# Routing list of a two-expert block: sums from TensorE, masks' inputs from ScalarE, fewer filler matmuls, and the accumulator filled from SBUF

## Chip, cores, metric

One NeuronCore of a Trainium2 chip (trn2). The metric is the device time in microseconds of one execution of the whole kernel; the time before is the median of three runs.

## What is computed

A block on x of 4 x 2048 tokens with 256 features: half a mixture of experts, attention, and half a mixture again.

```python
x = x + 0.5 * ffn(layernorm(x), router_w, wg, wu, wd)
x = x + attn(layernorm(x), Wq, bq, Wk, bk, Wv, bv, Wo, bo)
x = x + 0.5 * ffn(layernorm(x), router_w, wg, wu, wd)

def ffn(x, ...):                       # N = 8192 tokens, E = 8 experts, 2 per token
    capacity = int(1.25 * N / E)       # 1280 places per expert
    probs = softmax(xf @ router_w.T)
    topw, topi = top_k(probs, 2);  topw = topw / (topw.sum(-1) + 1e-6)
    order = lexsort((-fw, fe))         # by expert, the largest weight first
    rank = arange(2 * N) - starts[se]
    keep = rank < capacity
    disp[e, rank] = xf[token]          # kept tokens only
    eo = (silu(disp @ wg) * (disp @ wu)) @ wd
    out[token] += eo[e, rank] * weight * keep
```

The diff works on the step that says which tokens an expert keeps, and in which place of its list each stands.

## The kernel before

Each of the two mixtures runs in the same order: router, routing, lists, experts. The first mixture's router (`first_router`, L1156) runs over 16 groups of four tiles of 128 tokens: TensorE turns x and forms the logits, VectorE takes the statistics, GpSimd raises the variances to the power -0.5. `wrx`, the router's weights, is cleared by GpSimd (L1221) and filled by VectorE (L1232) ahead of the statistics on VectorE's queue. `choose` (L191) then takes each token's two experts, and writes their weights and factors into the columns behind x in `xw`. `write_rows` (L257) stores `xw` as `rows`, from which the experts gather.

`route` (L260) lays the weights of all experts out as 128 partitions of 512 tokens, 16 partitions to an expert (`wt`). Thirty rounds (L288 to L300) find each expert's smallest kept weight `cand` bit by bit: VectorE counts, TensorE sums the counts over the expert's partitions, VectorE takes the next value. What follows is a chain:

- L304 and L305 mark the tokens equal to the last kept weight (`tie`) and above it (`above`), and count both in each partition (`parts`).
- L307 and L308: TensorE sums the counts over the expert (`group`) and over its partitions further ahead (`ahead`).
- L310 scans the ties. L313 to L316 turn the sums into `need_t`, how many ties this partition keeps, and `off`, where its places begin.
- L317 to L320 drop the ties that have no place, scan what is kept, and make `St`, the place of each token.
- L323 `stay_busy` (L158): 14 calls of filler matmuls of 128 columns, whose result nobody reads. TensorE works in order, so L326, which turns `St` back to token-major, stands behind them.
- L328 to L335 split the place into `slot_hi` and `slot_lo`; L336 makes `behind_lo` on GpSimd, which ScalarE uses for the masks of the lists of experts 1 to 7.

The list of expert 0 is waited for (`RowList` with `waited_for`, L338). `high` (L351) compares `slot_hi` with 16 values (`hi`, L357) and multiplies by the row within the tile and by the tile (`hv`, L364 and L365), all on VectorE. `low` (L379) compares `slot_lo` with 128 values, eight tiles at a time (L384). TensorE multiplies the two (L396), ScalarE copies the sum (L404), TensorE turns it (L412), VectorE makes the indices, and GpSimd gathers the first rows (L470). The experts then keep TensorE busy to the end of the mixture, two chunks of 640 tokens to an expert.

In the first mixture `route` also carries other work between its rounds: the sums of expert 0's weights on GpSimd and the attention's weights.

The order of TensorE, VectorE and ScalarE is that of the program (`manual_schedule`); GpSimd's too, except among the experts. SP's queue is filled by a scheduler. Around the first routing it holds: 16 loads of x, expert 0's weights, the attention's weights, four copies of x to `acc` in HBM (L1245, 128 pieces of 64 KB), expert 1's weights, and the four writes of `rows` (L258). The experts add their results to `acc`. `hi` and `hv` take memory that `xw` gives up, so they wait for the writes of `rows`, which read it.

Of the kernel before, what the change touches and what calls it, by code (L numbers as in the profile page):

```python
# [9 lines left out]
F32 = mybir.dt.float32  # L10
F16 = mybir.dt.float16
# [16 lines left out]
def macaron_kernel(  # L28
# [103 lines left out]
    nc.gpsimd.memset(short, -(CAP - 1.0) / (P // E))  # L132
    minus_half = const.tile([P, 1], F32, name="minus_half")
    nc.gpsimd.memset(minus_half, -0.5)

    wr = const.tile([E, D], F32, name="wr")
    nc.scalar.dma_start(out=wr, in_=router_w)
# [122 lines left out]
    def route(w, pool, ppool, beside=iter(())):  # L260

        FULL = [P, GT * P]

        def new(name, dtype=F32):
            return pool.tile(FULL, dtype, name=name)

        def one(name, dtype=F32, n=1):
            return pool.tile([P, n], dtype, name=name)  # L270

        ps = ppool.tile([P, GT, P], F32, tag="turn", name="turn", bufs=1)
        by_group = w.rearrange("p e (g r) -> p r (e g)", r=GT)
        for r in range(GT):
            nc.tensor.transpose(ps[:, r, :], by_group[:, r, :], ident)
        wt = new("wt")
        nc.vector.tensor_copy(wt, ps.rearrange("p r q -> p (r q)"))

        cand, low, high = one("cand", I32), one("low", I32), one("high", I32)
        cand_f = cand.bitcast(F32)
        part = one("part", F16)
        above, tie = new("above", F16), new("tie", F16)
        nc.vector.memset(cand, 1 << 29)
        for bit in range(29, -1, -1):

            reach = ppool.tile([P, 4], F32, tag="cnt", name="reach", bufs=2)
            nc.tensor.matmul(reach[:, :1], group4, short, start=True, stop=False)  # L290
            nc.vector.tensor_scalar(above, wt, cand_f, 0.0, ALU.is_ge, ALU.add, accum_out=part)  # L291
            nc.tensor.matmul(reach[:, :1], group4, part, start=False, stop=True)
            next(beside, None)

            half = 1 << (bit - 1) if bit else 0
            nc.vector.tensor_scalar(low, cand, (1 << bit) | half, None, ALU.bitwise_xor)
            nc.vector.tensor_scalar(high, cand, half, None, ALU.bitwise_xor)
            nc.vector.tensor_scalar(  # L298
                cand_f, reach[:, :1], low.bitcast(F32), high.bitcast(F32), ALU.max, ALU.min
            )  # L300


        parts = one("parts", F16, 2)
        nc.vector.tensor_scalar(tie, wt, cand_f, 0.0, ALU.is_equal, ALU.add, accum_out=parts[:, 1:2])  # L304
        nc.vector.tensor_scalar(above, wt, cand_f, 0.0, ALU.is_gt, ALU.add, accum_out=parts[:, 0:1])  # L305
        cnt = ppool.tile([P, 4], F32, tag="cnt", name="all", bufs=2)
        nc.tensor.matmul(cnt[:, 0:1], group, parts[:, 0:1], start=True, stop=True)  # L307
        nc.tensor.matmul(cnt[:, 1:3], ahead, parts, start=True, stop=True)  # L308
        St = new("St")
        nc.vector.tensor_tensor_scan(St, row_of_ones, tie, 0.0, ALU.mult, ALU.add)  # L310
        nums = one("nums", n=3)
        need, need_t, off = (nums[:, k : k + 1] for k in range(3))
        nc.vector.tensor_scalar(need, cnt[:, 0:1], -1.0, float(CAP), ALU.mult, ALU.add)  # L313
        nc.vector.tensor_tensor(off, cnt[:, 2:3], need, ALU.min)
        nc.vector.tensor_tensor(need_t, need, cnt[:, 2:3], ALU.subtract)
        nc.vector.scalar_tensor_tensor(off, off, float(-1 - NOWHERE), cnt[:, 1:2], ALU.add, ALU.add)  # L316
        nc.vector.scalar_tensor_tensor(tie, St, need_t, tie, ALU.is_le, ALU.mult)  # L317
        nc.vector.tensor_tensor(above, above, tie, ALU.add)
        nc.vector.tensor_tensor_scan(St, row_of_ones, above, 0.0, ALU.mult, ALU.add)
        nc.vector.scalar_tensor_tensor(St, St, off, above, ALU.add, ALU.mult)  # L320


        stay_busy(ppool.tile([P, GT, P], F32, tag="turn", name="turn", bufs=1)[:, 0, :], 14, P)  # L323
        ps = ppool.tile([P, GT, P], F32, tag="turn", name="back", bufs=1)
        for r in range(GT):
            nc.tensor.transpose(ps[:, r, :], St[:, r * P : (r + 1) * P], ident)  # L326
        slot = pool.tile([P, E * T], I16, name="slot")
        nc.vector.tensor_scalar(  # L328
            slot.rearrange("p (q r) -> p q r", r=GT), ps.rearrange("p r q -> p q r"),
            float(NOWHERE), None, ALU.add,  # L330
        )
        nc.vector.tensor_scalar(
            slot_hi.rearrange("p e t -> p (e t)"), slot, 7, None, ALU.logical_shift_right
        )
        nc.vector.tensor_scalar(slot_lo.rearrange("p e t -> p (e t)"), slot, P - 1, None, ALU.bitwise_and)  # L335
        nc.gpsimd.tensor_scalar(behind_lo, slot_lo, -1.0, 0.5, ALU.mult, ALU.add)  # L336

    class RowList:  # L338

# [11 lines left out]
        def high(self):  # L351
            hi = self.pool.tile([P, T * HI], F16, tag="hi", name="hi", bufs=1)
            hv = self.pool.tile([P, 2 * T * HI], F16, tag="hv", name="hv", bufs=1)
            at = slot_hi[:, self.e, :]
            if self.waited_for:
                shape = [P, HI, T // TG, TG]
                nc.vector.tensor_tensor(  # L357
                    hi.rearrange("p (i g t) -> p i g t", g=T // TG, t=TG),
                    spread(counts[:, :HI, :].unsqueeze(2), shape),
                    spread(at.rearrange("p (g t) -> p g t", t=TG).unsqueeze(1), shape), ALU.is_equal,  # L360
                )
                hv = hv.rearrange("p (k i t) -> p k i t", k=2, t=T)
                shape, hi = [P, HI, T], hi.rearrange("p (i t) -> p i t", t=T)
                nc.vector.tensor_scalar(hv[:, 0, :, :], hi, row_in, None, ALU.mult)  # L364
                nc.vector.tensor_tensor(hv[:, 1, :, :], hi, spread(row_of.unsqueeze(1), shape), ALU.mult)  # L365
                self.hv = hv.rearrange("p k i t -> p t k i")
            else:
                shape, hi = [P, T, HI], hi.rearrange("p (t i) -> p t i", i=HI)
                nc.vector.tensor_tensor(
                    hi, spread(count[:, :HI].unsqueeze(1), shape), spread(at.unsqueeze(2), shape), ALU.is_equal  # L370
                )
                self.hv = hv.rearrange("p (t k i) -> p t k i", k=2, i=HI)
                nc.vector.tensor_scalar(self.hv[:, :, 0, :], hi, row_in, None, ALU.mult)
                nc.vector.tensor_tensor(self.hv[:, :, 1, :], hi, spread(row_of.unsqueeze(2), shape), ALU.mult)
# [837 lines left out]
    with tc.tile_pool(name="w1", bufs=2) as wpool:  # L1212
        weights, ws = {}, {}
        with tc.tile_pool(name="r1", bufs=1) as pool, tc.tile_pool(name="r1p", bufs=2, space=PSUM) as ppool:
# [5 lines left out]
            with tc.manual_schedule(engines=ENGINES):  # L1220
                nc.gpsimd.memset(wrx, 0.0)  # L1221
                ps = ppool.tile([P, DC, P], F32, tag="turn", name="wrT", bufs=1)
                for c in range(DC):
                    nc.tensor.transpose(ps[:, c, :E], wr[:, c * P : (c + 1) * P], ident[:E, :E])
                wrT = pool.tile([P, DC, E], F32, name="wrT")
                nc.vector.tensor_copy(wrT, ps[:, :, :E])
                ps = ppool.tile([P, DC, P], F32, tag="turn", name="means", bufs=1)
                for c in range(DC):
                    nc.tensor.matmul(ps[:, 0, :E], ones, wrT[:, c, :], start=(c == 0), stop=(c == DC - 1))
                mean = pool.tile([P, E], F32, name="wr_mean")  # L1230
                nc.vector.tensor_scalar(mean, ps[:, 0, :E], 1.0 / D, None, ALU.mult)
                nc.vector.tensor_tensor(  # L1232
                    wrx[:, :, :E], wrT, spread(mean.unsqueeze(1), [P, DC, E]), ALU.subtract
                )
                steps = attention_weights(pool, ppool)
                next(steps)
                first_router(xw, w, pool, ppool)
                for b in range(B):
                    write_rows(xw, rows[0], slice(b * NJ, (b + 1) * NJ))
                steps = chain(weight_sums(nc.gpsimd, 0, wpool, weights, ws, 0, 1), steps)  # L1240
                route(w, pool, ppool, steps)
                for _ in steps:
                    pass
        for b in range(B):
            nc.sync.dma_start(out=acc[b * N : (b + 1) * N, :], in_=x_in[b])  # L1245
        load_expert(1, wpool, weights)

        with tc.tile_pool(name="f1", bufs=1) as pool, tc.tile_pool(name="f1p", bufs=2, space=PSUM) as ppool:
# [55 lines left out]
```

## Time and profile before

| | |
|---|---|
| median of three runs | 1992.83 us (1991.80 to 1993.83) |
| the profiled execution's own time | 1991.23 us |
| its span | 1989.5 us |
| mean granted TensorE clock | 0.960 |
| first routing, from `choose` to the first gather | 35.5 to 110.8 us |
| second routing, to its first gather | to 1196.9 us |

Times within the profile count from the start of the span, in microseconds. PE is TensorE, PEld its weight loads, DVE VectorE, ACT ScalarE, POOL GpSimd, SP the queue that issues most DMAs. In the timeline a line gives start, duration, engine, line of the kernel, operation, output and inputs; in brackets stands how long the engine was idle before it, and what is taken to have released it. An f32 filler call appears as two matmuls.

### The profile page before, as it was taken

How to read it: one execution, taken by the hardware profiler on the slowest of the kernel's cores; microseconds unless marked ns; L12 is line 12 of the kernel's file. 1: busy time of each engine (PE TensorE's matmuls, PEld its weight loads, DVE VectorE, ACT ScalarE, POOL GpSimd, SP SyncE). 2: the span in 40 equal slices, each digit the busy share in tenths (PEclk: the TensorE clock that was granted, in tenths of full speed). 3: DMA queues.
4: the chain of work that ended last, by engine and by line, in shares of the span. 5: the costliest groups of instructions: out<-in, count | busy, mean ns of one | idle time of the engine just before them, and what ended most of it. 6: DMA issues, size and time to landing. Idle time of an engine off the chain costs nothing.

```text
span 1989.5 us, 25361 instructions
## 1 busy us (share of the span) xinstructions
PE 1843.9 (93%) x8812; PEld 1341.8 (67%) x8812; DVE 1386.9 (70%) x2539; ACT 922.4 (46%) x2269; POOL 1031.8 (52%) x1019
## 2 busy tenths in 40 slices
PE   6479999999999999999999528999999999999997
PEld 5347777777777777777888425777777777777776
DVE  7856767676767676647788885676767666676763
ACT  5045455555646463325444105554646373737332
POOL 4335555555555555535556324555555555555552
PEclk8589999999999999999999858999999999999999
DMA  9911323222222221125012541222222223232121
GB/s 339 332 30 28 92 34 86 59 61 71 50 71 49 71 50 28 28 25 172 25 40 89 187 142 29 71 50 71 49 71 50 71 50 79 41 95 30 31 29 19
DMA packets 99936, 148.85 MB, mean 75 GB/s; under 512 B 7512, under 2 KB 86368, under 8 KB 99680
## 3 DMA queue, kind: packets, MB, share of 16 engines
q1 hardware_dynamic: 69072, 103.29, 15.3%
q0 software_dynamic: 30720, 43.93, 13.8%
q8 instruction: 70, 1.15, 0.3%
q14 instruction: 58, 0.48, 0.1%
q10 hardware_dynamic: 16, 0.01, 0.0%
HBM read 99.49 MB, written 56.10 MB: 78 GB/s over the span
## 4 chain that ended last, share of the span: by engine, by line
PE 88%; DVE 6%; issue 3%; POOL 1%; ACT 1%; DMA 1%; POOLq 0%; DVEq 0%; ACTq 0%; SPq 0%
PE mm L561 49%; PE mm L764 23%; PE qp L949 2%; PE pc L1004 2%; PE tr L496 2%; PE py L1062 2%; PE back L716 2%; DVE above L291 2%; PE ix L396 1%; PE mm L822 1%; PE tr L1168 1%; DVE cand L298 1%; PE trq L992 1%; PE trx L941 1%; PE lg L1177 0%
## 5 line engine op out<-in xcount | busy, mean ns | idle before, releaser
L561 PE MATMUL mm<-xs,ws 128*128 128x320 f32 x1536 | 476.9, 433 | 2.8 <-DVE u L502 1.8
L505 POOL TENSOR_TENSOR ct<-ct 128x320 f32<-128x320 f32 x360 | 339.6, 943 | 187.9 <-DVE ct L592 164.4
L561 PEld LDWEIGHTS mm<-xs,ws 128*128 128x128 f32 x1536 | 284.3, 190 | 111.9 <-DVE u L502 2.9
L502 DVE TENSOR_TENSOR ct<-u,mm 128x640 f32<-128x640 f32 x256 | 209.9, 820 | 177.2 <-PE mm L561 166.0
L502 DVE TENSOR_TENSOR ct<-ct,mm 128x640 f32<-128x640 f32 x288 | 236.0, 819 | 73.7 <-PE mm L561 72.8
L470 POOL DMA_INDIRECT r<-rows,ixs x160 | 156.9, 981 | 235.2 <-ACT eo L697 172.8
L764 PE MATMUL mm<-ct,wds 128*128 128x320 f32 x960 | 278.1, 432 | 0.0
L589 ACT ACTIVATE ct<-ct 128x960 f32<-128x960 f32 (+2 forms) x192 | 141.7, 738 | 293.1 <-DVE ct L502 293.1
L390 ACT ACTIVATE lo<-from_below,behind_lo 128x129 f16<-128x129 f32 x896 | 272.9, 396 | 0.0
L764 PEld LDWEIGHTS mm<-ct,wds 128*128 128x128 f32 x960 | 179.2, 190 | 72.0 <-DVE ct L502 3.3
L764 PE MATMUL mm<-ct,wdt 128*128 128x320 f32 x720 | 213.5, 433 | 0.0
L698 POOL DMA_INDIRECT acc<-eo,ixs x80 | 127.7, 1596 | 142.9 <-ACT eo L697 124.9
L698 POOL DMA_INDIRECT out_dram<-eo,ixs x80 | 127.6, 1595 | 142.9 <-ACT eo L697 124.9
L561 PE MATMUL mm<-xsT,wgt 128*128 128x320 f32 x512 | 184.8, 443 | 0.0
L561 PE MATMUL mm<-xsT,wut 128*128 128x320 f32 x512 | 180.7, 435 | 0.0
L592 DVE TENSOR_TENSOR ct<-ct 128x640 f32<-128x640 f32 (+1 forms) x128 | 160.8, 1256 | 21.7 <-ACT ct L589 21.7
L502 DVE TENSOR_TENSOR u<-p,mm 128x640 f32<-128x640 f32 x128 | 105.1, 821 | 93.0 <-PE mm L561 80.6
L764 PEld LDWEIGHTS mm<-ct,wdt 128*128 128x128 f32 x720 | 132.1, 190 | 47.5
L561 PE MATMUL mm<-xsT,ws 128*128 128x320 f32 x512 | 158.7, 432 | 0.0
L598 ACT COPY p<-mm 128x640 f32<-128x640 f32 x128 | 88.4, 690 | 147.1 <-PE mm L561 147.1
L697 ACT ACTIVATE eo<-back,r 128x256 f32<-128x256 f32 x150 | 64.9, 478 | 152.7 <-PE back L716 152.7
L561 PEld LDWEIGHTS mm<-xsT,wut 128*128 128x128 f32 x512 | 97.7, 191 | 40.7 <-issue 0.8
(234 smaller groups left out, 2803.7 us busy)
## 6 DMA issues: line engine op xcount, KB each, us to landing
wgt<-in_L_ffn_wg_dram SPq DMA_DIRECT2D x16, 1024.0 KB, 4.9
wut<-in_L_ffn_wu_dram SPq DMA_DIRECT2D x16, 1024.0 KB, 7.2
wdt<-in_L_ffn_wd_dram SPq DMA_DIRECT2D x16, 1024.0 KB, 5.4
rows<-xw SPq DMA_DIRECT2D x7, 2240.0 KB, 19.4
xw<-in_L_attn_x_dram SPq DMA_DIRECT2D x16, 512.0 KB, 9.3
out_dram<-xw SPq DMA_DIRECT2D x16, 512.0 KB, 2.9
xw<-acc SPq DMA_DIRECT2D x15, 512.0 KB, 8.6
r<-rows,ixs POOLq DMA_INDIRECT x160, 2.8
```

Of the source, the lines that this page charges most:

```text
L291: nc.vector.tensor_scalar(above, wt, cand_f, 0.0, ALU.is_ge, ALU.add, accum_out=part)
L390: nc.scalar.activation(lo[:, t, :], from_below, AF.Sign, bias=at, scale=1.0)
L470: nc.gpsimd.indirect_dma_start(out=r, out_offset=None, in_=src[:, :], in_offset=bass.IndirectOffsetOnAxis(ap=lists[e][:, i : i + 1], axis=0),)
L502: nc.vector.tensor_tensor(o, a, b, op)
L505: nc.gpsimd.tensor_tensor(o, a, b, op)
L561: nc.tensor.matmul(ps, a, b, start=start, stop=True, skip_group_check=not start)
L589: nc.scalar.activation(h(p)[:, qs, :], h(p)[:, qs, :], AF.Silu)
L592: engine.tensor_tensor(h(p)[:, qs, :], h(p)[:, qs, :], hT(p)[:, qs, :], ALU.mult)
L598: nc.scalar.copy(p1, ps)
L697: nc.scalar.mul(eo, ps, got[k][i][:, D + e : D + e + 1])
L698: ins = nc.gpsimd.indirect_dma_start(out=dst[:, :], out_offset=bass.IndirectOffsetOnAxis(ap=lists[e][:, i0 + i : i0 + i + 1], axis=0), in_ ...
L764: nc.tensor.matmul(ps, a(p), b(p), start=(p == 0 and not more), stop=(p == NF - 1), skip_group_check=more)
```

## The change

- TensorE forms `need_t` and the start of the places outright: six one-column matmuls with negated matrices and constant columns instead of two. VectorE copies both numbers out and corrects `off` once.
- `stay_busy` makes 8 calls instead of 14.
- `behind_lo` and the first product of `hv` for the waited-for list go to ScalarE.
- `acc` is filled from `xw` in SBUF, in rows of 1 KB, instead of from x in HBM; on SP's queue these four DMAs keep their place, behind them come the four writes of `rows`, and then expert 1's weights.
- GpSimd makes five more constants at the start, ahead of `wrx`.

```diff
+    a_half = const.tile([P, 1], F32, name="a_half")
+    nc.gpsimd.memset(a_half, 0.5)
+    cap_part = const.tile([P, 1], F16, name="cap_part")
+    nc.gpsimd.memset(cap_part, CAP * E / float(P))
+    nowhere_part = const.tile([P, 1], F16, name="nowhere_part")
+    nc.gpsimd.memset(nowhere_part, (-1.0 - NOWHERE) * E / P)
+    minus_group = const.tile([P, P], F16, name="minus_group")
+    nc.gpsimd.tensor_scalar(minus_group, heads, -1.0, None, ALU.mult)
+    minus_ahead = const.tile([P, P], F16, name="minus_ahead")
+    nc.gpsimd.tensor_scalar(minus_ahead, ahead, -1.0, None, ALU.mult)
...
-        cnt = ppool.tile([P, 4], F32, tag="cnt", name="all", bufs=2)
-        nc.tensor.matmul(cnt[:, 0:1], group, parts[:, 0:1], start=True, stop=True)
-        nc.tensor.matmul(cnt[:, 1:3], ahead, parts, start=True, stop=True)
+        cnt = ppool.tile([P, 2], F32, tag="cnt", name="all", bufs=2)
+        for k, sums in enumerate((
+            ((group, cap_part), (minus_ahead, parts[:, 1:2]), (minus_group, parts[:, 0:1])),
+            ((group, nowhere_part), (ahead, parts[:, 1:2]), (ahead, parts[:, 0:1])),
+        )):
+            for n, (a, b) in enumerate(sums):
+                nc.tensor.matmul(cnt[:, k : k + 1], a, b, start=(n == 0), stop=(n == 2))
         St = new("St")
         nc.vector.tensor_tensor_scan(St, row_of_ones, tie, 0.0, ALU.mult, ALU.add)
-        nums = one("nums", n=3)
-        need, need_t, off = (nums[:, k : k + 1] for k in range(3))
-        nc.vector.tensor_scalar(need, cnt[:, 0:1], -1.0, float(CAP), ALU.mult, ALU.add)
-        nc.vector.tensor_tensor(off, cnt[:, 2:3], need, ALU.min)
-        nc.vector.tensor_tensor(need_t, need, cnt[:, 2:3], ALU.subtract)
-        nc.vector.scalar_tensor_tensor(off, off, float(-1 - NOWHERE), cnt[:, 1:2], ALU.add, ALU.add)
+        nums = one("nums", n=2)
+        need_t, off = (nums[:, k : k + 1] for k in range(2))
+        nc.vector.tensor_copy(nums, cnt)
         nc.vector.scalar_tensor_tensor(tie, St, need_t, tie, ALU.is_le, ALU.mult)
         nc.vector.tensor_tensor(above, above, tie, ALU.add)
+        nc.vector.scalar_tensor_tensor(off, need_t, 0.0, off, ALU.min, ALU.add)
         nc.vector.tensor_tensor_scan(St, row_of_ones, above, 0.0, ALU.mult, ALU.add)
         nc.vector.scalar_tensor_tensor(St, St, off, above, ALU.add, ALU.mult)
-        stay_busy(ppool.tile([P, GT, P], F32, tag="turn", name="turn", bufs=1)[:, 0, :], 14, P)
+        stay_busy(ppool.tile([P, GT, P], F32, tag="turn", name="turn", bufs=1)[:, 0, :], 8, P)
...
-        nc.gpsimd.tensor_scalar(behind_lo, slot_lo, -1.0, 0.5, ALU.mult, ALU.add)
+        nc.scalar.activation(behind_lo, slot_lo, AF.Identity, bias=a_half, scale=-1.0)
...
-                nc.vector.tensor_scalar(hv[:, 0, :, :], hi, row_in, None, ALU.mult)
+                nc.scalar.mul(hv[:, 0, :, :], hi, row_in)
...
                 first_router(xw, w, pool, ppool)
+                for t in range(0, T, NJ):
+                    nc.sync.dma_start(out=acc_tiles[:, t : t + NJ, :], in_=xw[:, t : t + NJ, 0:D])
                 for b in range(B):
                     write_rows(xw, rows[0], slice(b * NJ, (b + 1) * NJ))
...
-        for b in range(B):
-            nc.sync.dma_start(out=acc[b * N : (b + 1) * N, :], in_=x_in[b])
         load_expert(1, wpool, weights)
```

## The prediction

> **What bounds the kernel now.** I read the page's busy times and chain first, then the chain of waits and the timeline of the two stretches where the diff works, then the busy times by stage for clock and DMA.
>
> The page:
> ```profile
> PE 1843.9 (93%) x8812; PEld 1341.8 (67%) x8812; DVE 1386.9 (70%) x2539; ACT 922.4 (46%) x2269; POOL 1031.8 (52%) x1019
> PE 88%; DVE 6%; issue 3%; POOL 1%; ACT 1%; DMA 1%; POOLq 0%; DVEq 0%; ACTq 0%; SPq 0%
> ```
> TensorE carries 88% of the chain, but the experts and the attention, where it does, are not touched. The diff acts in the two routings, where VectorE and its hand-overs carry the chain. So the whole prediction is made in two stretches of some 15 us.
>
> The timeline of the first routing (start, duration, engine, line):
> ```profile
> 92.07 6.16 PE L161 MATMUL turn<-row_of_ones,ident 128*128 128x128 f32 x28
> 93.01 0.13 DVE L313 TENSOR_SCALAR nums<-all 128x1 f32<-128x1 f32 x1
> 93.44 0.74 DVE L317 SCALAR_TENSOR_TENSOR tie<-St,nums,tie 128x512 f16<-128x512 f32 x1
> 95.94 0.75 DVE L320 SCALAR_TENSOR_TENSOR St<-St,nums,above 128x512 f32<-128x512 f32 x1
> 98.29 0.66 PE L326 MATMUL back<-ident,St 128*128 128x128 f32 x4
> 98.98 0.69 DVE L328 TENSOR_SCALAR slot<-back 128x512 int16<-128x512 f32 x1 [2.29 <-PE back L326]
> 99.92 0.29 DVE L335 TENSOR_SCALAR slot_lo<-slot 128x512 int16<-128x512 int16 x1
> 100.29 0.62 POOL L336 TENSOR_SCALAR behind_lo<-slot_lo 128x512 f32<-128x512 int16 x1 [28.60 <-DVE slot_lo L335]
> 100.95 0.69 DVE L357 TENSOR_TENSOR hi<-counts,slot_hi 128x1024 f16<-128x1024 int16 x1 [0.75 <-POOL behind_lo L336]
> 101.68 0.49 DVE L364 TENSOR_SCALAR hv<-hi,row_in 128x1024 f16<-128x1024 f16 x1
> 102.08 0.69 DVE L365 TENSOR_TENSOR hv<-hi,row_of 128x1024 f16<-128x1024 f16 x1
> 103.42 4.93 PE L396 MATMUL ix<-lo,hv 128*32 128x128 f16 x64 [4.48 <-DVE lo L384]
> ```
> Two gaps. St is ready at 96.69, but the back transposes begin at 98.29, behind the 14 filler calls, which end at 98.23. And hi waits 0.75 us, by the label for GpSimd. The second routing corrects that label:
> ```profile
> 1180.18 4.88 PE L161 MATMUL turn<-row_of_ones,ident 128*128 128x128 f32 x28
> 1184.06 0.75 DVE L320 SCALAR_TENSOR_TENSOR St<-St,nums,above 128x512 f32<-128x512 f32 x1
> 1185.13 0.66 PE L326 MATMUL back<-ident,St 128*128 128x128 f32 x4
> 1187.13 1.18 POOL L336 TENSOR_SCALAR behind_lo<-slot_lo 128x512 f32<-128x512 int16 x1 [26.69 <-DVE slot_lo L335]
> 1187.13 0.69 DVE L357 TENSOR_TENSOR hi<-counts,slot_hi 128x1024 f16<-128x1024 int16 x1
> 1189.84 4.91 PE L396 MATMUL ix<-lo,hv 128*32 128x128 f16 x64 [4.06 <-DVE lo L384]
> ```
> Here hi starts together with behind_lo, so it does not wait for it. It waits for the rows' writes, whose source xw gives up the memory that hi takes: the last of the four was issued at 81.1 and took 19.7 us, so it landed at 100.8. The busy times by stage (PEclk, DMA share and GB/s are the last three columns) agree:
> ```profile
> 97.00:98.00 1.00, 1.00 (x7) 1.00 (x6) 0.00 (x0) 0.00 (x0) 0.00 (x0) 0.54 1.12 339
> 98.00:99.00 1.00, 0.89 (x6) 0.46 (x5) 0.02 (x1) 0.00 (x0) 0.00 (x0) 1.00 0.95 288
> 100.00:100.25 0.25, 0.00 (x0) 0.00 (x0) 0.20 (x2) 0.00 (x0) 0.00 (x0) 1.00 0.14 45
> ```
> The DMA engines run full to 99 us and are empty soon after 100: in the first routing a DMA backlog is the last gate.
>
> **The change, part by part.**
>
> *Numbers.* Four small VectorE operations between 93.01 and 93.44 become one copy. L313 to its dependent took 0.17, so tie starts 0.26 earlier. The new min/add (one column) sits between the sum into above and the second scan; such operations stood 0.07 to 0.11 apart, so +0.08. Net -0.18 per routing. TensorE's two one-column matmuls become six with six weight loads; two need nothing that is late, the other four at 0.1 us (a load of such weights) end about 92.6, under the first scan, which runs to 93.1.
>
> *Filler.* 14 calls made 28 matmuls of 0.22 us at half clock. Eight make 16, 3.5 us: from about 92.4 to 95.9, before St at 96.51. So the back transposes wait for St alone and start at 96.58. Their own time depends on the clock. At full clock four took 0.66. At half clock one took 0.47 and three 0.90 (L496 at 114.58 and 118.12), so four take 0.47 + 3 x 0.215 = 1.12. In the trace the grant came 5.9 us after the filler began in the first routing (97.9) and 3.2 us after it in the second (1183.4). [...]
>
> First routing: slot at 96.58 + 1.12 + 0.03 = 97.73 instead of 98.98, -1.25. Second: St at 1184.63, back at 1184.70, slot at 1185.85 instead of 1185.82, +0.03, since the early grant there had almost emptied the filler by itself.
>
> *The DMAs.* The four acc copies (8.4 MB) read SBUF instead of HBM in the same place of SP's queue, behind the attention weights (from about 37 us). The rows' four writes (9.2 MB) now stand ahead of expert 1's weights (3.15 MB). At the 345 GB/s that the rows' writes show, acc takes 24.3 us and the rows 26.6: they land at 88; taking 3.15 MB off the old landing gives 91.7. Both are well ahead of hi. With slot to hi 1.31 us as in the second routing, hi starts at 99.04 instead of 100.95: -1.91 in all there. The weights behind are done by 97 to 101, ahead of the gathers (108.6) and some 100 us ahead of expert 1. The rows also no longer wait for anything that is later than before: on SP they are passed by nothing.
>
> *ScalarE.* behind_lo leaves GpSimd, where nobody waited for it; on ScalarE it costs 0.72 (0.29 fixed with a per-partition operand, L390, plus 512 elements at 0.83 ns, L220), beside hi. hv's first product leaves VectorE. It stood 0.40 us on the path in the first routing and 0.65 in the second, where behind_lo ran on GpSimd at the same time and both were slower (0.73 against 0.49, 1.18 against 0.62). On ScalarE it takes 0.29 + 1024 x 0.83 ns = 1.14 from the end of hi, to hi + 1.9; VectorE's own path (hi, the other product, the first mask) lets TensorE start at hi + 2.07. The weight load must follow ScalarE by up to 0.3, so the bounds of the new wait are 0 and 0.15; I take 0.10. Behind the waiting load stand only the list's matmuls, which need it anyway; nothing else is due on ScalarE. From hi to the first ix matmul: 2.17 instead of 2.47 and 2.71.
>
> *GpSimd's set-up.* Five more operations ahead of wrx's memset: three at 0.03 and two of the 0.55 kind (L130), 1.2 us. wrx then comes at 7.9; TensorE's first use is at 8.41. VectorE's statistics shift by 1.2, rstd's last power from 33.7 to 34.9, and it is needed at 35.46. Cost nothing; without that cover 1.2.
>
> **Sum.** First routing: ix at 99.04 + 2.17 = 101.21 instead of 103.42, -2.21. Second: 1187.16 + 2.17 = 1189.33 instead of 1189.84, -0.51. Together -2.7 against the profiled execution: 1991.23 - 2.7 = 1988.5. That execution is 1.6 us below the median. Part is the lucky grant in the second routing: with the filler's end anywhere between 1184.87 (St) and 1186.34 (all at half clock), the usual one is some 0.5 later than the 1185.06 seen, and the changed kernel is free of that. So against the median -3.2: **1989.6 us**. The rest of the 1.6 I leave as scatter.
>
> **Rivals.**
> - *The clock is granted all the same* in both routings: another -0.92, 1988.7. For it: 3.2 us sufficed at 1183.4. Against: 5.9 at 97.9.
> - *The DMA gate stays*: the rows still land near 100.8. Then the first routing gains only 0.40 - 0.10, the second 1.0 with the 0.5 above: 1991.5. For it: the DMA engines have no free time before 99. Against: 3.15 MB leave the queue ahead.
> - *Slower: acc's writes in 1 KB pieces are slow.* They replace copies with 64 KB pieces, and the rows queue behind them. At half of 345 GB/s acc takes 48.7 us, the rows land at 112.4, hi waits until then, 11.6 later than before; less 1.3 gained elsewhere, 2003. It turns into a loss below about 210 GB/s (landing after 104). Against: the rows' 1.1 KB writes ran at 345.
> - *The set-up's cover is gone*: +1.2, 1990.8.
>
> **Numbers.** Forecast 0.54, clock granted 0.24, gate stays 0.11, cover gone 0.05, slow writes 0.06. The range takes in the first four with the runs' own scatter of 1 us: 1987.8 to 1992.0. Over 0.2% (4.0 us, about what a measurement can tell from no change) faster needs most of the clock case or scatter on the forecast: 0.33; slower 0.06; within 0.61.
>
> **What would show it.** In the changed profile: filler ended before St, back starting 0.07 behind it and taking 1.12 (0.66 in the rival); rows landed by 92 us and no wait ahead of hi; 2.1 to 2.2 from hi to ix in both routings; wrx later but ex still at 35.5. A gain outside the two routings, or hi still waiting at 100.9, would prove me wrong.

## The result and the profile after

The changed kernel takes **1987.85 us** (median of 11 runs, 1986.57 to 1988.22), the kernel before 1992.83 in 11 runs beside it (1990.70 to 1993.83): 0.9976 times, with the interval 0.9968 to 0.9984, or 5.0 us less. The prediction was 1989.6, with a range of 1987.8 to 1992.0: the result lies 0.05 us inside its lower end.

The profiled execution took 1988.04 us with a span of 1986.1. Its page, by the lines that were shown of before:
```profile
PE 1841.3 (93%) x8796; PEld 1338.2 (67%) x8796; DVE 1385.2 (70%) x2533; ACT 926.9 (47%) x2273; POOL 1030.9 (52%) x1022
PE 87%; DVE 8%; issue 2%; ACT 1%; POOL 1%; DMA 1%; POOLq 0%; DVEq 0%; ACTq 0%; SPq 0%
```
Little shows here: six VectorE instructions less, four more on ScalarE. 5 us of 1990 have to be looked for in the routings. The timeline of the first (the code around it stands 12 to 16 lines lower than before):
```profile
92.00 3.76 PE L173 MATMUL turn<-row_of_ones,ident 128*128 128x128 f32 x16
92.89 0.14 DVE L331 COPY nums<-all 128x2 f32<-128x2 f32 x1
93.06 0.75 DVE L332 SCALAR_TENSOR_TENSOR tie<-St,nums,tie 128x512 f16<-128x512 f32 x1
95.57 0.75 DVE L336 SCALAR_TENSOR_TENSOR St<-St,nums,above 128x512 f32<-128x512 f32 x1
96.47 1.09 PE L342 MATMUL back<-ident,St 128*128 128x128 f32 x4 [0.71 <-DVE St L336]
97.59 0.69 DVE L344 TENSOR_SCALAR slot<-back 128x512 int16<-128x512 f32 x1 [1.27 <-PE back L342]
98.90 0.72 ACT L352 ACTIVATE behind_lo<-slot_lo,a_half 128x512 f32<-128x512 int16 x1 [18.79 <-DVE slot_lo L351]
99.00 0.69 DVE L373 TENSOR_TENSOR hi<-counts,slot_hi 128x1024 f16<-128x1024 int16 x1 [0.19 <-DVE slot_lo L351]
99.73 0.69 DVE L381 TENSOR_TENSOR hv<-hi,row_of 128x1024 f16<-128x1024 f16 x1
99.78 1.15 ACT L380 ACTIVATE hv<-hi,row_in 128x1024 f16<-128x1024 f16 x1
100.97 0.46 PEld L412 LDWEIGHTS <-hv 128*32 128x32 f16 x9 [3.83 <-ACT hv L380]
101.07 4.92 PE L412 MATMUL ix<-lo,hv 128*32 128x128 f16 x64 [3.52 <-DVE lo L400]
```
Both gaps of before are gone. The filler ends at 95.76, ahead of `St`; `back` is released by `St` and nothing else; `hi` (99.00) starts behind `slot_lo` with no wait for memory. ScalarE's two operations lie beside VectorE's, and ix is released by VectorE's first mask `lo`, not by ScalarE. There is no room left, though: ix needs `hv` as weights, and their load, which waited for ScalarE, came at 100.97, 0.10 ahead of ix (0.03 in the second routing).

The second routing:
```profile
1177.88 3.76 PE L173 MATMUL turn<-row_of_ones,ident 128*128 128x128 f32 x16
1181.44 0.75 DVE L336 SCALAR_TENSOR_TENSOR St<-St,nums,above 128x512 f32<-128x512 f32 x1
1182.34 1.08 PE L342 MATMUL back<-ident,St 128*128 128x128 f32 x4 [0.70 <-DVE St L336]
1184.77 0.69 DVE L373 TENSOR_TENSOR hi<-counts,slot_hi 128x1024 f16<-128x1024 int16 x1
1186.85 4.92 PE L412 MATMUL ix<-lo,hv 128*32 128x128 f16 x64 [3.42 <-DVE lo L400]
```
The same picture: `back` behind `St` at half clock, ix 2.08 behind `hi`. The busy times by stage in the first routing (PEclk, DMA share and GB/s are the last three columns) answer to those of before:
```profile
95.00:96.00 1.00, 0.76 (x4) 0.46 (x3) 0.96 (x2) 0.00 (x0) 0.00 (x0) 0.50 0.77 245
96.00:97.00 1.00, 0.53 (x3) 0.56 (x4) 0.32 (x1) 0.00 (x0) 0.00 (x0) 0.50 0.10 32
97.00:98.00 1.00, 0.55 (x3) 0.15 (x1) 0.41 (x1) 0.00 (x0) 0.00 (x0) 0.50 0.00 0
```
The DMA engines are nearly empty from 96 on and empty from 97, expert 1's weights included; before, they were full to 99. The granted clock stays at 0.50.

For the comparison I measure each routing from its first scan of `St` (L310, now L328) to its first ix matmul, so that nothing from ahead of it is counted: 11.54 and 9.84 us before, 9.32 and 9.22 after.

### The profile page after: what moved, and what is told of

Read it like the earlier page. It is cut to its first block, busy times and chain, and to the rows that moved or that the text cites. A ratio compares the mean times of both kernels' runs of the same rounds, so it can differ in the third digit from the quotient of the medians.

```text
span 1986.1 us, 25337 instructions
## 1 busy us (share of the span) xinstructions
PE 1841.3 (93%) x8796; PEld 1338.2 (67%) x8796; DVE 1385.2 (70%) x2533; ACT 926.9 (47%) x2273; POOL 1030.9 (52%) x1022
## 4 chain that ended last, share of the span: by engine, by line
PE 87%; DVE 8%; issue 2%; ACT 1%; POOL 1%; DMA 1%; POOLq 0%; DVEq 0%; ACTq 0%; SPq 0%
PE mm L577 49%; PE mm L780 23%; DVE above L303 2%; PE qp L965 2%; PE pc L1020 2%; PE tr L512 2%; PE py L1078 2%; PE back L732 2%; PE ix L412 1%; PE mm L838 1%; DVE cand L310 1%; PE tr L1184 1%; PE reach L304 0%; PE trq L1008 0%; DVE st L1090 0%
```

## Experiments

None of these kernels leaves out work that the result needs, and one adds work that nobody reads. They ran on three chips. The experts' stages took 1494.2 to 1494.4 us in the profiles of before and after and in those of one chip (after_again, undo_filler, weights_first, undo_scalar), taken from the third `u` of a mixture to its last, or to the end, and 1497.3 to 1498.1 in those of the two others, whatever the kernel. So times of different chips are not set side by side; ratios are, each against the kernel before on the same chip. The table at the end of this section has all of them.

**The DMA part alone**, on the kernel before: `acc` from `xw`, and `rows` ahead of expert 1's weights.
```diff
                 first_router(xw, w, pool, ppool)
+                for t in range(0, T, NJ):
+                    nc.sync.dma_start(out=acc_tiles[:, t : t + NJ, :], in_=xw[:, t : t + NJ, 0:D])
...
-        for b in range(B):
-            nc.sync.dma_start(out=acc[b * N : (b + 1) * N, :], in_=x_in[b])
```


> Before, with acc filled from SBUF and the rows' writes ahead of expert 1's weights, nothing else. The medians stand 5.0 us apart, the two profiles 3.2 to 3.4. Gate theory (the rows usually land later than the 100.8 of the one profile before): hi no longer waits, the median falls by 2 us or more, and the scatter of the times shrinks. Filler theory (what the profile lacks is the filler ending later in usual executions): hi stands 1.3 us behind slot, the median falls by only 0.7 to 1.4.


Measured: 0.9999 (0.9990 to 1.0007), or -0.2 us (-2.0 to 1.4): the gate theory's fall of 2 us or more lies at the edge of the interval or beyond it, the other theory's 0.7 to 1.4 within it.
```profile
99.73 1.05 DVE L357 TENSOR_TENSOR hi<-counts,slot_hi 128x1024 f16<-128x1024 int16 x1 [0.19 <-DVE slot_lo L335]
```
Its first routing took 11.10 from scan to ix, 0.44 less than before, though the gate was gone: VectorE took `hi` 1.41 behind `slot`. Of the 0.44, 0.24 is a filler that ended earlier. And `hi` took 1.05, where before it took 0.69; the run that undoes ScalarE's part, below, shows why.

**All but the DMA part**: the changed kernel with the old copies of x and the old order of SP's queue (the diff above, reversed).


> After, with acc filled from HBM and the queue of before. Both theories: hi waits for the rows near 100.8 although slot is there at 97.7; the second routing gains 0.5 to 0.6 by the profile. Gate theory: the median stays 2 us or more above after (about 1990), with the wide scatter of before (3 us). Filler theory: 1.3 to 1.9 above after (about 1989.5), with the scatter of after (under 2 us).


Measured: 0.9987 (0.9981 to 0.9994). The timeline shows the gate, but at a small price:
```profile
98.15 0.69 DVE L344 TENSOR_SCALAR slot<-back 128x512 int16<-128x512 f32 x1 [1.27 <-PE back L342]
...
99.67 0.69 DVE L373 TENSOR_TENSOR hi<-counts,slot_hi 128x1024 f16<-128x1024 int16 x1 [0.30 <-DMA rows<-xw]
```
`hi` stands 1.52 behind `slot`, released by the rows' writes. Without a gate it is 1.41 in the first routing (after, dma_alone, before_again), so 0.11 is lost. In the profile of before it was 1.97, so 0.56. In this execution the DMA engines moved 54 GB/s from 98 to 99 and nothing in the microsecond behind it; in the profile of before they were full to 99. The last packet of the rows' writes ended at 99.0 here, at 99.3 and 99.5 in the two other profiles with the old transfers (before_again, filler_alone), and at 100.3 in the profile of before. So the gate varies from one execution to the next, and the one that the prediction read was long.

**The filler alone**: the kernel before with 8 calls.
```diff
-        stay_busy(ppool.tile(...)[:, 0, :], 14, P)
+        stay_busy(ppool.tile(...)[:, 0, :], 8, P)
```


> Before, with 8 filler calls instead of 14. Both theories: nothing gained in the first routing, since hi waits for the rows. Gate theory: 0 to 0.5 us off the median by the second routing, scatter as before. Filler theory: 1 to 1.5 us off the median, by the second routing, and less scatter. Back takes 1.1 us in both routings if the clock isn't granted, 0.66 if it is.


Measured: 0.9999 (0.9991 to 1.0008). Its profile gives 10.32 and 9.65 from scan to ix; `back` took 1.09 in the first routing and 0.63 in the second.
```profile
100.13 0.79 DVE L357 TENSOR_TENSOR hi<-counts,slot_hi 128x1024 f16<-128x1024 int16 x1 [0.46 <-DMA rows<-xw]
```
In the first routing `slot` came 6.08 behind the scan instead of 7.10, 1.02 earlier. `hi`, released by the rows' writes, stood 1.68 behind `slot`, so 0.27 of that was lost at the gate behind the filler. By the profile the part is still worth some 1.2 us there, which the times don't show (-1.8 to 1.6 us).

**The kernel before and the changed kernel once more**, to see what one profile is worth.


> The kernel before, profiled once more. Gate theory: hi in the first routing starts somewhere between 100.9 and 103, and the time of this execution follows it. Filler theory: hi at 100.9 within 0.3, and the start of back in the second routing moves within 1184.9 to 1186.4.

> The changed kernel on the chip of these runs, as their base. From the scan of the ties to the first ix matmul it took 9.3 and 9.2 us, the kernel before 11.5 and 9.8 in one profile and 11.5 and 10.8 in another. Theory (the two routings are all of it, 3.3 to 4.3 us): the median stands 3.3 to 4.3 below before, the intervals are 9.2 to 9.3 again. Rival (something outside the routings gives the rest of the 5.0): 5 below before again, and the gaps between chunks or the attention are shorter than in the profiles of before on the same chip.


Measured: 1.0004 (0.9996 to 1.0012) and 0.9977 (0.9968 to 0.9987). From scan to ix the kernel before took 11.50 and 10.79, the changed one 9.31 and 8.75. The first profile of before thus had a second routing 0.95 shorter than this one: its filler took 4.88 there, here 5.83, and the back transposes stood behind it both times, as the filler theory had it. And here the first routing had no gate:
```profile
99.28 0.69 DVE L328 TENSOR_SCALAR slot<-back 128x512 int16<-128x512 f32 x1 [2.45 <-PE back L326]
...
100.58 0.63 POOL L336 TENSOR_SCALAR behind_lo<-slot_lo 128x512 f32<-128x512 int16 x1 [28.75 <-DVE slot_lo L335]
100.69 1.06 DVE L357 TENSOR_TENSOR hi<-counts,slot_hi 128x1024 f16<-128x1024 int16 x1 [0.19 <-issue]
```
`hi` comes 1.41 behind `slot`, as soon as it can, but beside GpSimd it takes 1.06 instead of 0.69. Gate or contention: the first routing of before took 11.5 either way.

**Undo the filler**: the changed kernel with 14 calls; run twice.


> After, with 14 filler calls again. Filler theory: back starts behind the filler, 4.9 to 6.2 us after its start, so slot comes 0 to 1.2 us later in each routing by the clock's phase, back takes 0.66; the median rises by 0.6 to 1.6 and the times scatter more. Rival (the granted clock pays for the wait): no change within 0.4.

> After with 14 filler calls, profiled a second time: its first profile was the lowest of its own times (1987.6 of a median of 1992.0), so what the others lose isn't in it. In all ten profiles so far the clock's windows stand 3.413 us apart at one phase per execution, drawn anew each time, and the attention loses none, one or two whole windows at half clock (1.7 us each) by that phase. Theory of the phase: this profile shows slot up to 1.9 later behind the filler in one or both routings, or one or two lost windows in the attention, and these add up to the difference in span. Rival: the time is lost elsewhere, with fillers ended early and no lost window.


Measured: 1.0000 (0.9991 to 1.0008), and on another chip 0.9986 (0.9979 to 0.9992). The two do not agree. The profiles do: 9.24 and 9.71 from scan to ix, then 9.18 and 9.73, or some 0.5 longer than after in the second routing (1.0 longer than after_again) and nothing in the first. But the first profile was of the fastest of its 13 executions (1987.63, median 1991.95), so what the others lost isn't in it. The second has a span 4.9 longer: 3.7 of that lie in the experts' stages, which are longer on that chip in every kernel, 1.5 in the attention (last section), and nothing in the routings. The second routing of the later run:
```profile
1179.79 5.35 PE L173 MATMUL turn<-row_of_ones,ident 128*128 128x128 f32 x28
1183.35 0.75 DVE L336 SCALAR_TENSOR_TENSOR St<-St,nums,above 128x512 f32<-128x512 f32 x1
1185.20 0.66 PE L342 MATMUL back<-ident,St 128*128 128x128 f32 x4
```
`St` is ready at 1184.10; behind the filler `back` starts 1.10 later instead of 0.15, and the full clock returns 0.43 of that (0.66 instead of 1.09).

**No filler at all**: the changed kernel with 0 calls.


> After with no filler at all. Theory (8 calls end before St and are mostly too short for the clock): back starts at St all the same and takes 1.09 as without a grant, the routings as in after within 0.3 on average, median within 1 us of after's (4 below before). Rival (8 calls do bring the clock often enough): back at 1.09 always where after had 0.63 and 0.87 in two of four, 0.3 to 0.5 lost per routing.


Measured: 0.9983 (0.9975 to 0.9991), and 9.31 and 9.22 from scan to ix, as after.
```profile
97.08 1.09 PE L342 MATMUL back<-ident,St 128*128 128x128 f32 x4 [4.32 <-DVE St L336]
```
TensorE idles for 4.32 us, and `back` takes 1.09 (1.08 in the second routing), as in after. Against that profile the 8 calls buy nothing. But the profiles with 8 calls (eight of them, two routings each) have `back` at 0.63 in seven routings and at 1.08 or 1.09 in nine (at the 0.87 of the expectation in none); weights_first has 0.63 in both:
```profile
97.12 0.63 PE L342 MATMUL back<-ident,St 128*128 128x128 f32 x4 [0.95 <-DVE St L336]
```
So 8 calls bring the full clock in nearly half of the cases, at no wait. That is worth 0.45 each time, or 0.2 to a routing by this count; the times of no_filler and after can't tell it.

**Expert 1's weights first**: the changed kernel with its DMAs' sources, but the weights ahead of `acc` on SP's queue.
```diff
                 first_router(xw, w, pool, ppool)
+                load_expert(1, wpool, weights)
...
-        load_expert(1, wpool, weights)
```


> After, but with expert 1's weights issued ahead of acc and rows, as in before; acc still comes from SBUF. In after all DMAs were done at 96.0, so now the rows should land near 96. Theory of the edge (the rows need only land before 99): hi 1.4 behind slot, median unchanged within 0.5. The recorded step (the order is what lifts the gate): hi waits until 98 or more behind rows that land at 97.5 to 100.8, up to 1.8 lost.


Measured: 0.9978 (0.9969 to 0.9988), as the changed kernel beside it (0.9977). With the weights ahead the DMA engines are nearly empty from 95.2 on:
```profile
94.00:95.00 1.00, 1.00 (x7) 1.00 (x6) 0.97 (x4) 0.00 (x0) 0.00 (x0) 0.50 0.99 296
95.00:96.00 1.00, 1.00 (x7) 0.98 (x6) 1.00 (x1) 0.00 (x0) 0.00 (x0) 0.61 0.20 64
```
The last write of the rows landed at 96.8 and `hi` started at 99.19, 1.41 behind `slot`. So the new order isn't needed to take the rows off the path. Their last packets ended at 88.9 in after, at 96.2 here, and at 99.0 to 100.3 in the four profiles with the old transfers: the order is worth some 7 us, and the source in SBUF, with the weights' place ahead of `acc`, some 3 or more, which suffices. The order with `acc` still copied from HBM was not run. A higher rate while `acc` is filled, from 40 to 60 us, is not what the source brings: the engines moved 354 GB/s in after and only 315 in before, but 354 in before_again and 361 in all_but_dma, with the old copies.
```profile
40.00:60.00 20.00, 2.47 (x19) 1.92 (x20) 17.43 (x54) 0.00 (x0) 11.22 (x9) 0.50 1.05 354
40.00:60.00 20.00, 2.47 (x19) 1.92 (x20) 17.43 (x54) 0.00 (x0) 10.67 (x8) 0.50 1.07 361
```
The first line is of after, the second of all_but_dma.

**Undo ScalarE's part**: behind_lo back on GpSimd, hv's first product back on VectorE.
```diff
-        nc.scalar.activation(behind_lo, slot_lo, AF.Identity, bias=a_half, scale=-1.0)
+        nc.gpsimd.tensor_scalar(behind_lo, slot_lo, -1.0, 0.5, ALU.mult, ALU.add)
...
-                nc.scalar.mul(hv[:, 0, :, :], hi, row_in)
+                nc.vector.tensor_scalar(hv[:, 0, :, :], hi, row_in, None, ALU.mult)
```


> After, with behind_lo back on GpSimd and hv's first product back on VectorE. By the recorded sum: from hi to the first ix matmul 2.45 to 2.5 in the first routing or 2.7 where behind_lo runs beside it, against 2.07 in after, so 0.4 to 0.65 lost per routing, 0.8 to 1.3 in all. Rival (ScalarE's own path had cost it again): no change.


Measured: 1990.38 beside the changed kernel's 1987.87 on the same chip, or 0.9991 of before (0.9984 to 0.9997). The first routing:
```profile
98.74 0.63 POOL L352 TENSOR_SCALAR behind_lo<-slot_lo 128x512 f32<-128x512 int16 x1 [27.32 <-DVE slot_lo L351]
98.84 1.06 DVE L373 TENSOR_TENSOR hi<-counts,slot_hi 128x1024 f16<-128x1024 int16 x1 [0.19 <-DVE slot_lo L351]
99.93 0.49 DVE L380 TENSOR_SCALAR hv<-hi,row_in 128x1024 f16<-128x1024 f16 x1
100.33 0.68 DVE L381 TENSOR_TENSOR hv<-hi,row_of 128x1024 f16<-128x1024 f16 x1
```
`hi` starts at once and runs 1.06; ix starts at 101.67, 2.83 behind `hi` instead of 2.07. In the second routing it is 2.71 instead of 2.08. In the profile of before the gate held up `hi` (100.95) until behind_lo was over (100.91), so this price was not to be seen there. That also explains the DMA part alone: without the gate `hi` started earlier and took 1.05.

**Undo the numbers**: `cnt` and `nums` as before, all else changed.


> After with need_t and off made on VectorE again from two matmuls. By the recorded sum 0.18 lost per routing, 0.4 in all, which the times can't tell; from the end of the ties' scan to the start of tie on VectorE 0.35 instead of 0.09 in the profile. Rival (the four more matmuls or the copy out of PSUM had eaten that): the interval from scan to St the same as in after.


Measured: 0.9985 (0.9978 to 0.9991).
```profile
92.03 1.22 DVE L324 TENSOR_TENSOR_SCAN St<-row_of_ones,tie 128x512 f32<-128x512 f32 x1
96.09 0.75 DVE L334 SCALAR_TENSOR_TENSOR St<-St,nums,above 128x512 f32<-128x512 f32 x1
```
From the scan to the end of `St` it takes 4.81, and 4.57 after (from 91.75): 0.24 to a routing. The times can't tell so little.

**More set-up on GpSimd**: four more 128 x 128 products that nobody reads, ahead of the router's weights.
```diff
+    spare = const.tile([P, P], F16, name="spare")
+    for _ in range(4):
+        nc.gpsimd.tensor_scalar(spare, heads, -1.0, None, ALU.mult)
```


> After with four more products of 128x128 on GpSimd at the start, ahead of wrx, whose result nobody reads: 2.2 us. By the recorded cover (TensorE needs wrx at 8.41, rstd is due at 35.46) the change's own 1.2 us was free; with 3.4 in all wrx comes at 10.1 and TensorE's logits wait 1.7, rstd's last power ends near 37. Theory: ex starts 1.5 to 1.8 later, at 36.6 to 37.2, and the median rises as much. Rival (the stage is held by x's arrival): ex at 35 to 36 as before.


Measured: 0.9974 (0.9963 to 0.9984), no loss. But it did not test what it was meant to:
```profile
7.91 0.17 POOL L1241 MEMSET wrx<- 128x64 f32 x1
8.07 1.76 POOL L150 TENSOR_SCALAR spare<-heads 128x128 f16<-128x128 f32 x3
```
The compiled program puts the clearing of `wrx` ahead of three of the four, so it came only 0.5 later than in the changed kernel (7.40). The cover holds for that much; where it ends was not found.

**All together.** The third column is the time of both routings by the profile, each from its first operation on `wt` to the third product `u` of the experts behind it, less the mean of the two profiles of before (176.95 and 177.93, mean 177.4). The second is the ratio less 1, times 1993 us.

| kernel | times against before, us | routings by one profile, us |
|---|---|---|
| before_again | +0.8 (-0.8 to 2.4) | +0.5 |
| after | -4.8 (-6.4 to -3.2) | -3.8 |
| after_again | -4.6 (-6.4 to -2.6) | -2.9 |
| dma_alone | -0.2 (-2.0 to 1.4) | -0.9 |
| filler_alone | -0.2 (-1.8 to 1.6) | -1.3 |
| all_but_dma | -2.6 (-3.8 to -1.2) | -3.4 |
| undo_filler | 0.0 (-1.8 to 1.6) | -2.9 |
| undo_filler_2 | -2.8 (-4.2 to -1.6) | -3.0 |
| no_filler | -3.4 (-5.0 to -1.8) | -3.0 |
| undo_numbers | -3.0 (-4.4 to -1.8) | -3.6 |
| undo_scalar | -1.8 (-3.2 to -0.6) | -1.2 |
| weights_first | -4.4 (-6.2 to -2.4) | -4.2 |
| more_setup | -5.2 (-7.4 to -3.2) | -3.5 |

With one exception the routing of a single profile lies within the interval of the times. The exception is the first run with 14 calls; its repeat on another chip agrees with its profile. What cost the first its 2.9 us isn't known; its profile, of its fastest execution, can't show it.

## Why the prediction was right, and which terms were off

**The sum held.** Forecast were -2.7 against the profiled execution and -3.2 against the median. From scan to ix, the two profiles of before take 21.38 and 22.29 (both routings), the two of after 18.54 and 18.06: -3.5 by the means. Over the whole routing stretches it is 177.4 - 174.1 = -3.3. The ratios give -4.8 and -4.6 with intervals that reach to -3.2 and -2.6. So the mechanism and the size in the routings were right, while the median, 5.0 us down for 3.2 forecast, fell just inside the range, and the gain of over 0.2% that came had been given the smaller chance, 0.33. Whether the 1.5 us or so that the routings leave over are more than scatter stays open; the clock in the next paragraph, and stretches at half clock in the attention (last section), are candidates.

**Filler: right. Clock: right in this profile, in part by luck.** `back` starts 0.15 behind the end of `St` (0.07 forecast) and takes 1.09 and 1.08, for 1.12. But half clock in both routings was the author's choice, which the two grants in the trace of before (5.9 and 3.2 us behind the filler's start) do not settle, and it was too sure: with eight calls the rival "clock granted" came in seven of 16 routings. The forecast put its gain at nothing; by that count it is 0.2 to a routing. The two profiles show what came ahead of a grant, in stretches between moments at which the clock can be seen to change (last section). In before TensorE was busy for 2.49 of the 3.41 us from 91.10 on and the clock stayed at half; it was busy all through the next stretch, and the clock was full from 97.93. In after it was busy for 2.67 and 2.44 of the stretches from 90.99 and 94.40, and the clock stayed at half behind both:
```profile
91.10:94.51 3.41, 2.49 (x13) 2.49 (x13) 3.34 (x11) 0.00 (x0) 0.00 (x0) 0.50 1.12 346
94.51:97.93 3.42, 3.42 (x18) 3.42 (x17) 2.12 (x3) 0.00 (x0) 0.00 (x0) 0.50 1.12 345
90.99:94.40 3.41, 2.67 (x16) 2.61 (x16) 3.34 (x10) 0.00 (x0) 0.00 (x0) 0.50 1.04 385
94.40:97.81 3.41, 2.44 (x11) 1.78 (x9) 2.10 (x3) 0.00 (x0) 0.00 (x0) 0.50 0.45 142
```
The first two lines are of before, the others of after. What the calls are worth in this place, the rows answer: with no calls TensorE paused for 4.32 and `back` took the 1.09 of after, while with 14 calls, which leave no such pause, `back` starts 0.95 later in the second routing and the clock returns 0.43.

**Numbers: right**, 0.24 for 0.18 to a routing. From the scan, `tie` starts 1.31 later instead of 1.56 (0.25, for 0.26), and from there to the end of `St` it is 3.26 as against 3.25: the new min/add cost 0.01, not 0.08.

**ScalarE: the mechanism right, the size wrong.** The step "From hi to the first ix matmul: 2.17 instead of 2.47 and 2.71" gave 0.30 and 0.54. ScalarE's durations came as worked out (0.72 and 1.15), but the wait taken at 0.10 was 0, the lower bound: the lag of up to 0.3 for the weight load was the author's estimate, and in after the load came 0.05 behind ScalarE's product in both routings. And 2.47 was no fair "before": undone on its own, the part costs 0.76 and 0.63, 1.4 us for 0.84 and, by the profiles, the largest single part (the medians on that chip stand 2.5 apart). The term that was left out is that GpSimd's behind_lo lengthens VectorE's `hi` from 0.69 to 1.06 when it starts 0.10 ahead of it; that is 0.37 of the 0.76. The trace of before showed the two start together in the second routing, but there `hi` took 0.69 and it was hv that took 0.73; in the first the gate kept them apart.

**The DMA gate: a term of the sum that was too large, and the reason only half right.** The prediction had 0.65 of gate in the first routing and let the rows land earlier by their place in the queue. The rows did land early: their last write was issued at 68.9 and took 20.6, so 89.5, for 88 to 91.7. But the order was not needed (weights_first). The gate was 0.56 and not 0.65: `hi` stands at least 1.41 behind `slot` in the first routing, for which the prediction took the 1.31 of the second. This miss of 0.10 and ScalarE's wait of 0.10 that didn't come cancel, so that the first routing's 2.21 came out to within 0.01 in part by luck. And the gate's worth differs by execution: 0.56 in the profile of before, none in before_again, 0.11 in all_but_dma. In before_again the changed kernel's gain of 2.2 in the first routing stands against no gate at all: there the filler's end and GpSimd beside `hi` make it up. The rival "the DMA gate stays", at 1991.5, had the same fault: it left a gain of 1.3 us, and all_but_dma, with the old transfers, gained 2.6 (1.2 to 3.8; 3.4 by its profile).

**The rivals that failed.** Slow writes: the engines moved 354 GB/s from 40 to 60 us, where 210 was the prediction's estimate of the point of loss. Cover gone: `wrx` was cleared at 7.40, the last power of rstd ended at 34.39 (34.9 forecast), and `ex` started at 35.36, before 35.46.

**The 0.5 for the lucky grant** in the second routing was a fair guess and rather small: before_again took 0.95 longer there.

**Where one part's gain went.** The DMA part alone and the filler alone gave nothing that the times could show (0.9 and 1.3 by their profiles), where all parts together gave 4.8. Filler and gate stood in a row ahead of `hi`, and beside `hi` stood GpSimd. Take the gate away and VectorE meets GpSimd (0.36 in dma_alone); take the filler away and it meets the gate (0.27 in filler_alone). That much the profiles show; that it explains all of the difference is not shown.

## What to carry to other kernels

A wait in a chain that several things end at nearly the same time is worth little until all of them are moved; price such edits together, and look for what the next in line is (here, first a filler, then a DMA, then another engine's operation beside it). A gate can also cover a contention: an operation that is held up looks short, and its price shows only when it starts on time (`hi` took 0.69 behind the gate in the profile of before, and 1.06 without it in before_again). Fourteen filler calls ahead of four small transposes cost more in waiting than the full clock gave back in one routing (0.95 against 0.43), and about as much in the other (9.24 and 9.18 from scan to ix, against 9.32 with eight); eight, which end before the transposes' input is ready, cost no wait and brought the full clock in seven of 16 routings. That is to be measured for each place.

## What was not expected of the hardware

**GpSimd beside VectorE.** A 128 x 512 operation on GpSimd from int16 to f32 lengthened VectorE's two-input int16 `hi` from 0.69 to 1.06 when it came 0.10 ahead of it, and took 0.63 itself. Started with `hi` it took 1.18, `hi` stayed at 0.69, and the next operation, hv, took 0.73 instead of 0.49.

**The clock changes on a grid.** In each of the six profiles whose clock was followed through the routings and the attention (before, after, undo_filler_2, no_filler, undo_numbers, more_setup) it changes at moments that are a whole number of 3.413 us apart, with one phase to an execution: before, at 97.93, 101.34, 108.17, 1183.36 and 1190.19, for example. TensorE has short gaps in the attention, and a stretch of 3.41 us at half clock came behind some of them and not behind others. In undo_numbers TensorE was busy for 1.53 of the 3.41 us from 948.36 on, and the stretch from 951.77 to 955.18 ran at half clock. In before it was busy for 1.28 of the 3.41 us from 947.85 on, with no gap of over 1.45 us, and the clock was half from 951.26 to 954.67; later, busy for 1.66 of those from 1053.66 on, with a gap of 1.77, it kept the full clock. In after 1.64 from 1050.14 on were followed by half clock from 1053.55 to 1056.96. What decides between the last two is not shown. The first line is of undo_numbers, the next two are of before, the last is of after:
```profile
948.36:951.77 3.41, 1.53 (x11) 1.30 (x12) 2.81 (x9) 3.15 (x8) 2.31 (x3) 1.00 0.00 0
947.85:951.26 3.41, 1.28 (x10) 0.81 (x9) 3.27 (x10) 3.15 (x8) 1.90 (x3) 1.00 0.00 0
1053.66:1057.08 3.42, 1.66 (x11) 1.00 (x9) 2.85 (x9) 2.57 (x6) 1.69 (x3) 1.00 1.07 353
1050.14:1053.55 3.41, 1.64 (x12) 1.10 (x11) 2.83 (x8) 3.07 (x7) 1.59 (x4) 1.00 1.08 349
```
From the last `u` of the first mixture to the second `wt` the profiles took 266.5 to 267.1 (three), 268.3 to 268.8 (nine) or 270.3 us (two). The busy times by stage of a profile with two such stretches at half clock (undo_numbers), and then of one that kept the full clock in both places (undo_filler):
```profile
950.00:956.00 6.00, 5.32 (x22) 4.34 (x21) 1.85 (x7) 2.43 (x5) 2.37 (x4) 0.72 0.00 0
1056.00:1062.00 6.00, 4.93 (x21) 4.13 (x22) 2.69 (x9) 3.93 (x9) 3.01 (x4) 0.72 0.26 81
```
```profile
950.00:956.00 6.00, 6.00 (x35) 5.31 (x35) 2.23 (x6) 1.75 (x5) 0.88 (x2) 1.00 0.00 0
1056.00:1062.00 6.00, 6.00 (x36) 5.31 (x35) 3.52 (x11) 0.95 (x2) 2.53 (x7) 1.00 0.26 90
```
The mean clock falls from 1.00 to 0.72, with 21 or 22 matmuls in the stretch instead of 35 or 36 (the stage lies 1.6 us later in the first, so the stretches don't hold quite the same work). Each such stretch at half clock costs about 1.7 us (the steps between 266.8, 268.5 and 270.3), as much as most of the parts tried here. That such stretches are what spreads the single times of one kernel over 5 us is likely, but was not shown. The clocks on record point that way: of the 53 executions of the kernel before on the last chip, the six with a mean granted clock of 0.959 took 1997.5 us in the mean, the 25 with 0.960 took 1996.0, and the eleven with 0.962 took 1994.3; in which stage the clock was half isn't recorded. How often each kernel has one can't be told from one profile each.
